# Widening the base product of a LoRA-MoE kernel from two groups of four batches to all eight batches at once

## The chip, the cores and the metric

The kernel runs on one core of one Trainium2 chip. The metric is the time of one execution on the device, in microseconds (us). Times of several runs are given as a median with the lowest and the highest.

In the profile PE is TensorE (matrix products), PEld its loads of the stationary operand, DVE is VectorE, ACT is ScalarE, POOL is GpSimd and SP is SyncE, which issues most DMAs (SPq is its queue). An instruction is named by its line of the kernel, its engine and operation, and the tile it writes and the tiles it reads.

## The reference, cut to what matters

Eight batches of 256 tokens with 1024 features go through a matrix that each batch chooses for itself, and then through a base layer with a mixture of low-rank adapters; the input is added at the end.

```python
def reference(x, ids, cond_weight, base_W, base_b, router_W, router_b, A, B, expert_map):
    y = einsum('bsi,boi->bso', x, cond_weight[ids])          # (8, 256, 1024), own 1024x1024 matrix per batch
    base_out = einsum('btd,od->bto', y, base_W) + base_b     # one 1024x1024 matrix for all
    probs = softmax(einsum('btd,nd->btn', y, router_W) + router_b)   # 15 choices
    topk_p, topk_i = top_k(probs, 8)
    w = einsum('btk,btke->bte', topk_p, onehot(expert_map[topk_i], 8))
    h = einsum('btd,erd->bter', y, A)                        # 8 experts of rank 16: 128 values
    lora = einsum('bter,eor->bto', h * w[..., None], B) * 2.0
    return x + base_out + lora
```

All data is fp32.

## The kernel before

Both large products are computed with Winograd's form of Strassen's scheme: a product of two 2x2 block matrices with seven block products in place of eight, at the price of sums and differences of blocks.

**Stage 1** (lines 265 to 540) makes y = x times the chosen matrix, one batch per round `b`. In a round one level of the scheme is used: seven calls of `block` (L287), each of four matmuls with 512 columns, into the PSUM tiles `pa`, `pb` and `pc`. `turns` (L388) makes the differences of x on VectorE, `first_sum` to `fourth_sum` those of the weights. Results are evicted into `m0` and `m1` (views of the buffer `late`), turned in 32x32 blocks by `flip` (L242, VectorE), and brought into their place in `y` by `moves` (L299): 16 copies on ScalarE for each of `m0` and `m1`. In a round the copies of `m0` run at once; those of `m1` are put in the deque `behind` and run in the next round. `project(b - 1)` (L129) computes the router's logits and h of the batch before: 16 matmuls with `y` as stationary operand, then a list of VectorE and ScalarE steps (`logits`, `softmax`, `top`, two `route_to`, `weigh`), whose result is `hw`; `turn` (L250) carries it into `hwT` with 16 ScalarE copies. `prepare` (L325) makes the block sums of the base matrix and stores them in DRAM as `left_raw` and `left_sum`; `load_left(n)` (L206) loads the n-th of seven sets back into two tiles of the pool `wpool`, which has eight.

**Stage 2** (lines 545 to 818) makes base_out + lora + x with two levels of the scheme. The outer level has seven products, each of which is an inner level of seven blocks. The batches are taken in two groups `g` of four; in each group the outer quarters of y are (half of the features) x (two batches), and an inner quarter has 256 tokens: one batch. So there are 14 products, each called through `product` (L597), and each of their matmuls has 256 columns.

A product issues seven blocks in a fixed order, `pa` (a11 b11), `pc` (s1 t1), `pa` (s2 t2), `pb` (a12 b21), `pa` (s3 t3), `pc` (s4 b22), `pa` (a22 t4), where blocks two, four, six and seven also take a matmul with the adapter term (`up`, `hwT`) in four of the seven products. After a block, `take` evicts the accumulator with its base added (on VectorE, or on ScalarE with the bias `bb` where there is no base) or `plus` adds it to an earlier result. The tiles `pa`, `pb` and `pc` have two buffers of one PSUM bank each. In the last product `pa` is split over two tiles, `pa` and `pe`, one for each half of the rows.

Ahead of each block stands a `gap(n)`: steps listed for it in `gaps`, and then `fill(2)`, which takes two steps from the deque `soon`, or from `later` if `soon` is empty. These deques carry VectorE's side work: the four `differences` (L218) of the next product, the outer sums (`first_terms`, `outer`), the joint sums, and the additions of the residual x with the stores of results. Within a stage PE, VectorE, ScalarE and SP issue in the order in which the program is written; a wait of one instruction holds all behind it on its engine. How the end of stage 1 and the start of stage 2 are interleaved on one engine is left to the scheduler.

The outer terms of a group are made out of place: `t2` is a tile of its own. `load_left` is called in gap 5, two products ahead. The projection of batch 7 stands between the second and the third product, in the tile `pe`.

Of the kernel before, what the change touches and what calls it, by code (L numbers as in the profile page):

```python
# [28 lines left out]
def kernel(  # L29
# [4 lines left out]
    xr: bass.AP,  # L34
    ids: bass.AP,
# [23 lines left out]
    assert ER == P and E == 8 and B % GB == 0  # L59
# [4 lines left out]

    tpool = ctx.enter_context(tc.tile_pool(name="t", bufs=6))
# [24 lines left out]
    yv = [y.rearrange("p i h j q k s -> p i h q j k s") for y in ys]  # L90
# [10 lines left out]
    v = late[:, lo : lo + 8 * S].rearrange("p (i j k t) -> p i j k t", i=2, j=2, k=2)  # L101
# [27 lines left out]
    def project(b, ph, order=(0, 1)):  # L129
# [4 lines left out]
        for j in order:  # L134
            for k in range(KC):
                nc.tensor.matmul(  # L136
                    ph[:, j, : ER + N],
                    lhsT=y[:, k // KH, th, k % KH // 2, bi, k % 2, ts(j, P)],
                    rhs=ar_sb[:, k, :],
                    start=(j == order[0] and k == 0),  # L140
                    stop=(k == KC - 1),
                    skip_group_check=True,
                )
# [73 lines left out]

    def differences(right):  # L218

        b11, b12, b21, b22 = right[:, 0, 0], right[:, 0, 1], right[:, 1, 0], right[:, 1, 1]  # L220
        t = {}

        def minus(n, of, less):
            def run():
                t[n] = tpool.tile([P, 2 * S], F32, name="tt").rearrange(
                    "p (k o) -> p k o", k=2
                )
                x, y = (t[v] if isinstance(v, int) else v for v in (of, less))
                nc.vector.tensor_sub(t[n], x, y)
                return t[n]  # L230

            return run

        return [minus(1, b12, b11), minus(2, b22, 1), minus(3, b22, b12), minus(4, b21, 2)]


    lefts = [0, 1, 3, 5, 4, 6, 2] * (B // GB)
# [27 lines left out]
    with ExitStack() as phase:  # L265
        xpool = phase.enter_context(tc.tile_pool(name="x", bufs=2))
        prep = phase.enter_context(tc.tile_pool(name="prep", bufs=1))
        ps = phase.enter_context(
# [30 lines left out]
        def moves(b, oh, m):  # L299


            y = ys[b // GB][:, oh, b % GB // 2, b % 2].rearrange(
# [132 lines left out]
        for b in range(B):  # L435
# [30 lines left out]
            def by_s4():  # L466
# [3 lines left out]
                run(moves(b, 0, m0))  # L470
# [47 lines left out]
            else:  # L518
                left[0] = load_left(lefts[0])
                terms = [step() for step in differences(yv[0][:, 0, 0])]  # L520
# [8 lines left out]
                left[1] = load_left(lefts[1])  # L529
# [3 lines left out]
            behind = moves(b, 1, m1)  # L533
# [11 lines left out]
    with ExitStack() as phase:  # L545

        mpool = phase.enter_context(tc.tile_pool(name="m2", bufs=1))
        qpool = phase.enter_context(tc.tile_pool(name="q2", bufs=6))
        xpool = phase.enter_context(tc.tile_pool(name="x2", bufs=1))
        places_x = [xpool.tile([P, 2, S], F32, name=f"xt{n}") for n in range(2)]  # L550
        places_x += [
            ms[:, o, h].rearrange("p (m t) -> p m t", m=2) for o in range(2) for h in range(2)
        ]
        loaded = 0
        ps = phase.enter_context(
            tc.tile_pool(name="ps", bufs=2, space=bass.MemoryType.PSUM)
        )
        ps_e = phase.enter_context(
            tc.tile_pool(name="ps_e", bufs=1, space=bass.MemoryType.PSUM)
# [4 lines left out]
        add, sub = nc.vector.tensor_add, nc.vector.tensor_sub  # L564


        soon, later = deque(), deque()
        steps_of = steps

        def fill(n):  # L570
            for _ in range(n):
                if soon or later:
                    soon.popleft()() if soon else later.popleft()[1]()

        def block(acc, left, right, first, up=None, hw=None):

            for mi in range(2):
                for k in range(2):
                    nc.tensor.matmul(  # L579
                        acc[mi][:, mi, :],  # L580
                        lhsT=left[:, 2 * k + mi, :],
                        rhs=right[:, k, :],
                        start=(first and k == 0 and (mi == 0 or acc[0] is not acc[1])),
                        stop=(up is None and k == 1),
                        skip_group_check=True,
                    )
                if up is not None:
                    nc.tensor.matmul(  # L588
                        acc[mi][:, mi, :],
                        lhsT=up[:, ts(mi, P)],  # L590
                        rhs=hw,
                        start=False,
                        stop=True,
                        skip_group_check=True,
                    )

        def product(left, terms, right, base, into, done, gaps, u=None, hw=None, split=False):  # L597
# [6 lines left out]
            b11, b12, b21, b22 = right[:, 0, 0], right[:, 0, 1], right[:, 1, 0], right[:, 1, 1]  # L604
            t1, t2, t3, t4 = terms

            def plus(dst, acc, other):
                if acc[0] is acc[1]:
                    add(dst, acc[0], other)  # L609
                else:  # L610
                    for mi in range(2):
                        add(dst[:, mi], acc[mi][:, mi], other[:, mi])

            def take(dst, acc, i, j):
                if isinstance(base, int):
                    for mi in range(2):
                        c = base + 2 * i + mi
                        nc.scalar.activation(  # L618
                            dst[:, mi], acc[mi][:, mi], AF.Identity, bias=bb[:, c : c + 1]
                        )  # L620
                else:
                    plus(dst, acc, base(i, j))

            def term(i, j):
                if u is None:
                    return ()
                if (i, j) == (0, 1):
                    return upd[:, u, :], hw[:, 1, :]
                return up[:, u, i, :], hw[:, j, :]

            def gap(n):
                for step in gaps.get(n, ()):
                    step()
                fill(2)

            pa = 2 * [ps.tile([P, 2, S], F32, name="pa")]
            pb = 2 * [ps.tile([P, 2, S], F32, name="pb")]
            pc = 2 * [ps.tile([P, 2, S], F32, name="pc")]
            if split:

                pa[1] = ps_e.tile([P, 2, S], F32, name="pe")
# [4 lines left out]
            gap(1)  # L646
# [5 lines left out]
            gap(3)  # L652
            block(pb, a12, b21, True, *term(0, 0))
            plus(c[0, 0], pb, c[0, 0])
# [3 lines left out]
            plus(c[1, 1], pa, c[1, 1])  # L658
            done(1, 1, c[1, 1])
            gap(5)  # L660
            block(pc, s4, b22, False, *term(0, 1))
            plus(c[0, 1], pc, c[0, 1])
            done(0, 1, c[0, 1])
            gap(6)
# [3 lines left out]
            fill(len(soon))  # L668
            while later and later[0][0] not in (c[0, 1], c[1, 0]):
                later.popleft()[1]()  # L670
            done(1, 0, c[1, 0])

        def fresh(i, j):
            return qpool.tile([P, 2, S], F32, name="q")
# [4 lines left out]
        for g in range(B // GB):  # L679
            y, hw = yv[g], hwTs[g]  # L680
            end = g == B // GB - 1
            b11, b12, b21, b22 = y[:, 0, 0], y[:, 0, 1], y[:, 1, 0], y[:, 1, 1]
            u = mpool.tile([P, 2, 2, 2, S], F32, name="u")
            t2 = mpool.tile([P, 2, 2, 2, S], F32, name="t2")
            xs = {}

            def number(oh, th, i, j):
                return ((g * 2 + oh) * 2 + th) * 4 + 2 * i + j

            def load_x(*r):  # L690
                nonlocal loaded
                xs[r] = places_x[loaded % len(places_x)]
                loaded += 1
                nc.sync.dma_start(xs[r].rearrange("p m t -> p (m t)"), xr[number(*r)])

            def finish(oh, th):


                def done(i, j, q):
                    x, n = xs[oh, th, i, j], number(oh, th, i, j)  # L700

                    def run():
                        add(q, q, x)
                        nc.sync.dma_start(outq[n], q.rearrange("p m t -> p (m t)"))

                    later.append((q, run))

                return done

            def joint(i, j, q):  # L710


                def run():
                    add(q, v[:, i, j], q)

                soon.append(lambda: add(u[:, i, j], u[:, i, j], q))
                later.append((q, run))
                finish(1, 1)(i, j, q)

            def last(i, j, q):  # L720
                if (i, j) == (1, 0):
                    for mi in range(2):
                        nc.sync.dma_start(outq[number(1, 0, 1, 0), :, ts(mi, S)], q[:, mi])
                else:
                    finish(1, 0)(i, j, q)

            def at(t):
                return lambda i, j: t[:, i, j]

            def update(dst, x, z, quarters=((0, 0), (0, 1), (1, 0), (1, 1))):  # L730
                return [
                    (lambda i=i, j=j: sub(dst[:, i, j], x[:, i, j], z[:, i, j]))
                    for i, j in quarters
                ]

            def first_terms(*quarters):

                for q in quarters:
                    soon.extend(update(b11, b12, b11, [q]))
                    soon.extend(update(t2, b22, b11, [q]))  # L740

            seven = [

                (b11, 0, at(u), nothing),
# [139 lines left out]
```

## Time and profile before

| | |
|---|---|
| median of 3 runs | 433.87 us (433.84 to 434.34) |
| the profiled execution | 434.09 us, of which the profile's span is 432.3 us |
| TensorE busy | 426.6 us, 99% of the span |
| VectorE busy | 328.6 us, 76% |
| ScalarE busy | 167.0 us, 39% |
| DMA | 106.05 MB, mean 245 GB/s |
| stage 2 on TensorE | from 228.23 us to the end |

The span is shorter than the execution's time, since something lies around it. A matmul record's duration holds its way through the array as well, so the spacing of records, and not their duration, tells what they cost. A row of the timeline or the chain has start, duration, engine, line, operation and count; in square brackets stands how long the engine was idle before and what ended it. In the groups by form the columns after the bar are busy us, mean ns of one, and idle time before.

### The profile page before, as it was taken

Reading aid. Unit: us, or ns where it says so; the run is one execution under the profiler, and the core shown is the slowest. Engines: PE = TensorE matmul, PEld = TensorE weight load, DVE = VectorE, ACT = ScalarE, POOL = GpSimd, SP = SyncE. Lnnn points to the kernel's source line nnn. Section 1 sums busy time; section 2 is a strip of 40 time slices with the busy share of each in tenths; the row PEclk is TensorE's granted clock in tenths of the full one; section 3 lists DMA queues with packets and bytes.
Section 4 is the critical chain, followed back from the end, with each engine's and each line's share of the span. In section 5 each row is a group of like instructions: output and inputs, shape, how many; then the busy total and the mean of one; then the engine's idle time right before and its main releaser. Section 6 shows DMA issues by size and latency. Waiting matters only on the chain.

```text
span 432.3 us, 4927 instructions
## 1 busy us (share of the span) xinstructions
PE 426.6 (99%) x1642; PEld 293.6 (68%) x1642; DVE 328.6 (76%) x556; ACT 167.0 (39%) x458; POOL 0.7 (0%) x6
## 2 busy tenths in 40 slices
PE   8999999999999999999999999999999999999997
PEld 5344464644646446455458898888888888888886
DVE  0699999986878898998885777946597858745595
ACT  1019377965758657776838231200201100000200
POOL 0000000000000000000000000000000000000000
DMA  7996997869687598792759942523967725912843
GB/s 265 416 351 264 345 331 294 303 223 324 217 299 281 208 338 312 257 316 86 242 231 371 370 143 104 201 91 110 378 211 273 284 73 202 392 48 69 296 159 133
DMA packets 32779, 106.05 MB, mean 245 GB/s; under 512 B 3058, under 2 KB 6898, under 8 KB 29554
## 3 DMA queue, kind: packets, MB, share of 16 engines
q1 hardware_dynamic: 32610, 105.21, 66.9%
q10 hardware_dynamic: 144, 0.52, 0.4%
q8 instruction: 13, 0.21, 0.2%
q14 instruction: 12, 0.10, 0.1%
HBM read 84.49 MB, written 21.23 MB: 245 GB/s over the span
## 4 chain that ended last, share of the span: by engine, by line
PE 96%; DMA 2%; SPq 1%; issue 0%; DVE 0%
PE pa L290 24%; PE pa L579 22%; PE pc L290 13%; PE pc L579 11%; PE pb L290 7%; PE ph L136 6%; PE pb L579 6%; PE pc L588 3%; DMA wt<-in_wq_dram 2%; PE pb L588 2%; PE pa L588 1%; PE pe L136 1%; PE pe L579 1%; SPq L359 0%; DMA ids_sb<-in_ids_dram 0%
## 5 line engine op out<-in xcount | busy, mean ns | idle before, releaser
L308 ACT COPY y<-late 32x256 f32<-32x256 f32 x256 | 103.0, 402 | 41.9 <-DVE late L244 38.9
L579 PE MATMUL pa<-tt,wt 128*128 128x256 f32 x324 | 78.1, 380 | 0.0
L579 PEld LDWEIGHTS pa<-tt,wt 128*128 128x128 f32 x324 | 61.3, 190 | 8.9 <-DVE u L609 0.3
L290 PE MATMUL pa<-wt,x 128*128 128x512 f32 x128 | 57.5, 593 | 0.4 <-DMA wt<-in_wq_dram 0.4
L290 PE MATMUL pa<-wt,tt 128*128 128x512 f32 x120 | 54.0, 593 | 0.0
L618 ACT ACTIVATE q<-pa,bb 128x256 f32<-128x256 f32 x12 | 5.0, 471 | 104.9 <-PE pa L579 104.0
L290 PEld LDWEIGHTS pa<-wt,x 128*128 128x128 f32 x128 | 24.2, 190 | 30.7 <-issue 30.4
L290 PEld LDWEIGHTS pa<-wt,tt 128*128 128x128 f32 x120 | 22.3, 190 | 26.1 <-issue 25.9
L255 ACT COPY hwT<-late 32x64 f32<-32x64 f32 x128 | 31.1, 243 | 18.7 <-DVE late L244 17.1
L136 PEld LDWEIGHTS ph<-late,y 128*128 128x128 f32 x224 | 28.4, 189 | 3.3 <-issue 3.3
L290 PE MATMUL pb<-wt,x 128*128 128x512 f32 x64 | 29.1, 595 | 1.0 <-DMA wt<-in_wq_dram 1.0
L290 PE MATMUL pc<-wt,x 128*128 128x512 f32 x64 | 28.9, 594 | 0.0
L290 PE MATMUL pc<-wt,tt 128*128 128x512 f32 x64 | 28.8, 592 | 0.0
L136 PE MATMUL ph<-late,y 128*128 128x143 f32 x224 | 28.6, 284 | 0.0
L579 PE MATMUL pc<-tt,wt 128*128 128x256 f32 x112 | 27.8, 379 | 0.0
L405 DVE TENSOR_TENSOR wt<-wt 128x2048 f32<-128x2048 f32 (+1 forms) x9 | 18.4, 2047 | 7.9 <-PE pa L290 5.5
L579 PE MATMUL pc<-y,wt 128*128 128x256 f32 x96 | 24.0, 379 | 0.0
L579 PE MATMUL pb<-y,wt 128*128 128x256 f32 x96 | 24.0, 379 | 0.0
L290 PEld LDWEIGHTS pb<-wt,x 128*128 128x128 f32 x64 | 12.0, 190 | 17.0 <-issue 14.4
L579 PEld LDWEIGHTS pc<-tt,wt 128*128 128x128 f32 x112 | 21.3, 190 | 2.9
L290 PEld LDWEIGHTS pc<-wt,x 128*128 128x128 f32 x64 | 12.1, 190 | 15.5 <-issue 14.8
L290 PEld LDWEIGHTS pc<-wt,tt 128*128 128x128 f32 x64 | 12.1, 190 | 15.3 <-issue 14.6
(118 smaller groups left out, 548.4 us busy)
## 6 DMA issues: line engine op xcount, KB each, us to landing
wt<-in_wq_dram SPq DMA_DIRECT2D x28, 1024.0 KB, 5.6
wt<-left_raw SPq DMA_DIRECT2D x14, 1024.0 KB, 6.2
wt<-left_sum SPq DMA_DIRECT2D x14, 768.0 KB, 7.9
out_dram<-q SPq DMA_DIRECT2D x31, 256.0 KB, 2.3
x<-in_xq_dram SPq DMA_DIRECT2D x7, 1024.0 KB, 6.9
late<-in_xr_dram SPq DMA_DIRECT2D x20, 256.0 KB, 6.7
wt<-in_wq_dram SPq DMA_DIRECT2D x8, 512.0 KB, 7.9
spare<-in_bq_dram SPq DMA_DIRECT2D x4, 1024.0 KB, 5.0
```

The source lines that it names most:

```text
L136: nc.tensor.matmul(ph[:, j, : ER + N], lhsT=y[:, k // KH, th, k % KH // 2, bi, k % 2, ts(j, P)], rhs=ar_sb[:, k, :], start=(j == order[0] ...
L255: lambda a=a, r=r: nc.scalar.copy(to[32 * r : 32 * r + 32, :, a, :], hw[32 * a : 32 * a + 32, :, ts(r, 32)],)
L290: nc.tensor.matmul(acc, lhsT=right[:, k, :], rhs=left[:, k, :], start=(first and k == 0), stop=(k == KH - 1), skip_group_check=True,)
L308: lambda a=a, r=r: nc.scalar.copy(y[32 * r : 32 * r + 32, :, :, a, :], m[32 * a : 32 * a + 32, :, :, r, :])
L405: nc.vector.tensor_add(q["s1"][:, h], q["a21"][:, h], q["a22"][:, h])
L579: nc.tensor.matmul(acc[mi][:, mi, :], lhsT=left[:, 2 * k + mi, :], rhs=right[:, k, :], start=(first and k == 0 and (mi == 0 or acc[0] is n ...
L588: nc.tensor.matmul(acc[mi][:, mi, :], lhsT=up[:, ts(mi, P)], rhs=hw, start=False, stop=True, skip_group_check=True,)
L618: nc.scalar.activation(dst[:, mi], acc[mi][:, mi], AF.Identity, bias=bb[:, c : c + 1])
```

## The change

Stage 2 takes all eight batches at once. The outer quarters are now (half of the features) x (four batches), an inner quarter has 512 tokens (two batches), and there are 7 products whose matmuls have 512 columns. The layout of y puts two batches of an inner quarter next to each other (256 elements each) so that a quarter is one run of 512 for each k. Five further things follow or go with it:

- The outer sums are made in place in y: T2 = b22 - b12 + b11 in b12, T3 = T2 - b11 in b11, T4 = b21 - T2 in b21, then b22 - T2 in b12. The order of the outer products changes accordingly, and so do where their results lie (`u`, `v`) and at which of them the bias enters: in the fifth product it is added with the base in one `scalar_tensor_tensor` for each half.
- PSUM: `pa` has two buffers of two banks, `pb` and `pc` have one of two banks each.
- The differences use tiles of `wpool` (two in one tile) in place of a pool of their own. The four of the first product, issued in stage 1's last round, have 1024 elements in place of 512.
- In the last round of stage 1 only ten of the sixteen copies of `m0` run at once. The other six and the sixteen of `m1` run in gaps 1, 2 and 3 of the first product (6, 5 and 11), and the projection of batch 7 stands in gap 5 of the first product, in the second `pa` buffer. The `turn` copies of batches 6 and 7 run in gap 0 of the third product.
- `load_left` is called in gap 0 of the product before. Residuals come in pieces of 512 KB into three tiles; each is asked for (`ask`) when an earlier one has been added. The last block is issued as 512 columns for the first half of the rows and twice 256 for the second, and evicted and stored in those three pieces.

The diff, cut to its core:

```diff
-    yv = [y.rearrange("p i h j q k s -> p i h q j k s") for y in ys]
+    yv = [y.rearrange("p h j i k b s -> p h j i k b s") for y in ys]
...
-                t[n] = tpool.tile([P, 2 * S], F32, name="tt").rearrange(
-                    "p (k o) -> p k o", k=2
-                )
+                if n % 2:
+                    t["two"] = wpool.tile([P, KH, OH], F32, name="wt")
+                t[n] = t["two"][:, ts((n - 1) % 2, 2)]
...
-    lefts = [0, 1, 3, 5, 4, 6, 2] * (B // GB)
+    lefts = [0, 1, 3, 4, 6, 5, 2]
...
-                run(moves(b, 0, m0))
+                behind.extend(moves(b, 0, m0))
+                run(behind, 10 if last else None)
...
-                terms = [step() for step in differences(yv[0][:, 0, 0])]
+                terms = [step() for step in differences(yv[0][:, 0])]
...
-                left[1] = load_left(lefts[1])
...
+        W = 2 * S
...
+        def block(acc, left, right, first, up=None, hw=None, pieces=(1, 1)):
             for mi in range(2):
+                for n in range(pieces[mi]):
+                    at = ts(n, W // pieces[mi])
+                    for k in range(2):
+                        nc.tensor.matmul(
+                            acc[:, mi, at],
+                            lhsT=left[:, 2 * k + mi, :],
+                            rhs=right[:, k, at],
...
+                    else:
+                        nc.vector.scalar_tensor_tensor(
+                            dst[:, mi], acc[:, mi], c, base(i, j)[:, mi], ALU.add, ALU.add
                         )
...
+        def gap(n, more=0):
             for step in gaps.get(n, ()):
                 step()
+            fill(3 if more and u is not None else 2)
...
+            pa = ps_a.tile([P, 2, W], F32, name="pa")
+            pb = ps_b.tile([P, 2, W], F32, name="pb")
+            pc = ps_b.tile([P, 2, W], F32, name="pc")
...
+            if end is not None:
+                fill(len(soon) + len(later))
+                block(pa, a22, t4, False, *term(1, 0), (1, 2))
+                end(pa)
+                return
...
+        def end(pa):
+            dst = u[:, 1, 0]
+            for mi, cut in ((0, ds(0, W)), (1, ds(0, S)), (1, ds(S, S))):
+                add(dst[:, mi, cut], pa[:, mi, cut], dst[:, mi, cut])
+                nc.sync.dma_start(
...
+        b11, b12, b21, b22 = (y[:, h] for h in range(2) for y in yv)
+        hw1, hw2 = hwTs
+        seven = [
+            (b11, None, 0, at(u), nothing),
+            (b21, at(u), None, fresh, finish(0, 0), 0, hw1),
+            (b12, at(u), None, at(u), nothing),
+            (b22, at(u), None, at(v), nothing, 2, hw2),
+            (b11, at(u), KH, at(u), nothing),
+            (b12, None, None, fresh, joint, 1, hw2),
+            (b21, at(u), None, at(u), finish(1, 0), 1, hw1),
+        ]
+        sums = {
+            0: update(b12, sub, b22, b12, [0]) + update(b12, add, b12, b11, [0]),
+            2: update(b11, sub, b12, b11),
+            3: update(b21, sub, b21, b12) + update(b12, sub, b22, b12),
+        }
+        def project_last():
+            ph = ps_a.tile([P, 2, W], F32, name="pa")[:, 0].rearrange("p (j o) -> p j o", j=2)
+            (logits, *rest), last_waiting = project(B - 1, ph)
+            soon.appendleft(logits)
+            soon.extend(update(b12, sub, b22, b12, [1]) + update(b12, add, b12, b11, [1]))
+            soon.extend(rest)
...
+            if not last:
+                gaps[0].append(lambda m=n + 1: left.update({m: load_left(lefts[m])}))
...
+            if n == 0:
+                for k, count in ((1, 6), (2, 5), (3, 11)):
+                    gaps[k].append(lambda count=count: run(behind, count))
+                gaps[5].append(project_last)
+            if n == 1:
+                gaps[0] += 3 * [ask]
+                ps_a.tile([P, 2, W], F32, name="pa")
+            if n == 2:
+                gaps[0].append(lambda: run(turn(*waiting)))
+                gaps[0].append(lambda: run(turn(*last_waiting)))
```

## The prediction, made before the changed kernel was run

> **What bounds the kernel now.** I read the page first (busy times and the chain that ended last), then the chain in order of time, the busy times by stage, the waits of the weight loads, the groups with shapes kept apart, and last the timelines of single engines round the edit.
>
> ```profile
> span 432.3 us, 4927 instructions
> ...
> PE 426.6 (99%) x1642; PEld 293.6 (68%) x1642; DVE 328.6 (76%) x556; ACT 167.0 (39%) x458; POOL 0.7 (0%) x6
> ...
> PE 96%; DMA 2%; SPq 1%; issue 0%; DVE 0%
> ```
>
> TensorE is busy 99% and carries 96% of the chain. Nothing else sets the end, so a gain must come out of PE's own instructions, its few stalls, or the tail.
>
> ```profile
> 220.88 3.43 PE pa L290 x8
> 224.31 3.92 PE ph L136 x32
> 228.23 1.73 PE pa L579 x8
> ```
>
> This is the chain in order of time (start, us, what) where stage 1 ends. Eight records of a matmul with 512 columns take 3.43 us, eight with 256 take 1.73. Stage 2, the part that is rewritten, begins at 228.23.
>
> ```profile
> core 0: us, PE busy (x) PEld busy (x) DVE busy (x) ACT busy (x) POOL busy (x), PEclk, DMA share, GB/s
> 228.23:429.30 201.07, 201.03 (x944) 176.58 (x943) 141.50 (x254) 29.88 (x88) 0.00 (x0) 1.00 0.56 206
> ```
>
> Busy times in stage 2: PE has no idle time, the clock is 1.00, VectorE is busy 141.5 of 201 us, the DMA engines 56%.
>
> ```profile
> PEld pa L579 <- DVE u L609: 0.3, 1, 0.3
> PEld pa L579 <- DVE late L609: 0.2, 1, 0.2
> ```
>
> These are all the waits of PE's loads in stage 2: 0.5 us, both behind VectorE evictions. In the PE timeline three blocks are late by 0.07, 0.10 and 0.08 us for them, 0.25 in all.
>
> **The change on PE.** Every matmul is two records. Before, stage 2 has 14 products of 28 matmuls (784 records) and eight products with 8 extra matmuls (128 records): 912 records of 256 columns. The second product runs from 240.15 to 255.69, 72 records, so 0.2158 us each: 196.8 us. After, there are 7 products on twice the columns: 456 records, of which the last half block is cut in two: 450 of 512 columns and 12 of 256. A stage-1 round has 56 records of 512 columns from 112.82 to 136.85 without its projection, 0.4291 each. Sum 193.1 + 2.6 = 195.7. The pairing saves 1.1 us and no more: the array's work is the same. The projection of batch 7 (3.93 us from 255.69) moves from between two products into the first product and costs the same. Before, 201.04 us of chain minus 3.93 and 196.8 leaves 0.31 of stalls and seams; after, if nothing stalls, PE ends at 228.23 + 3.93 + 195.7 = 427.9 instead of 429.27: 1.4 less.
>
> **What the other engines must deliver.** A block is 3.43 us, or 5.15 with the outer-term matmuls; call the products P0 to P6. P0 with the projection runs 228.2 to 256.2, P1 to 287.1, P2 to 311.1, P3 to 342.0, P4 to 366.0, P5 to 396.9, P6 to 427.9.
>
> ```profile
> L579 PEld LDWEIGHTS pa<-tt,wt 128*128 128x128 f32 x324 | 61.3, 190 | 8.9 <-DVE u L609 0.3 <-DVE late L609 0.2
> L405 DVE TENSOR_TENSOR wt<-wt 128x1024 f32<-128x1024 f32 x2 | 2.5, 1225 | 2.4 <-DMA wt<-in_wq_dram 2.3
> ```
> ```profile
> 230.72 0.69 DVE L732 TENSOR_TENSOR t<-y 128x512 f32<-128x512 f32 x1
> 231.33 0.68 DVE L732 TENSOR_TENSOR y<-y 128x512 f32<-128x512 f32 x1
> ```
>
> Weight loads (190 ns in the groups by form) already hide in a 216 ns record, so halving them gains nothing. VectorE starts independent 512-wide operations 0.61 us apart; with 512 elements more at the slope between 685 ns (512) and 1225 ns (1024), a 1024-wide one occupies 1.14, or 1.25 when it needs the one before. Stage 2 after has 41 evictions (four takes and three additions in each of seven products, less the eight takes of P0 and P5 that ScalarE does), 24 differences, 20 in-place outer sums (16 such units before), 8 joint sums, 16 residuals: 109 units, 124 us against 129 for some 214 half-size ones now. All of it lies beside PE if the order fits: three units per 3.43 us block are 3.42, four per 5.15 us block are 4.6. I replayed the queue. P2 is tightest: last take of P1 to 288.4, two differences 290.8, take 291.9 (wanted at 293.9), two more, a take, two sums, take 298.9 (wanted at 300.8), addition 305.5 (wanted at 307.7). So 1.9 us of cover; without it each late microsecond is a microsecond of PE. In P4 the take becomes two scalar_tensor_tensor of 512, an operation without a row: I take 0.65 each from the 512-wide row, with 1.4 us of cover; at twice that it costs 0.8 us. Below nothing is excluded: no PE instruction waits for a take that comes earlier.
>
> Moved steps. The four first differences, in stage 1's last round, grow from 0.61 to 1.14 each: VectorE is then 2.2 us later from 213, and its 2.00 us idle before 217.55 (PE's third-sum block) takes that up. Their two wpool tiles come free at 207 to 211 by PE's blocks; if one comes from the a21 tile (read until 217.4), the last block of stage 1 waits 1.3 us.
>
> ```profile
> 223.12 6.61 ACT L308 COPY y<-late 32x256 f32<-32x256 f32 x16 [7.83 <-DVE late L244]
> ...
> 231.72 0.84 ACT L618 ACTIVATE u<-pc,bb 128x256 f32<-128x256 f32 x2 [0.46 <-PE pc L579]
> ...
> 234.31 5.78 ACT L308 COPY y<-late 32x256 f32<-32x256 f32 x14
> ```
>
> Batch 7's projection now needs all its copies on ScalarE (0.413 us apart). Ten of the first sixteen stay before 228; takes with bias grow to 0.55 per half. Take to 232.5, 6 copies 235.0, take 236.1, 5 copies 238.1, take 239.3, 11 copies 243.9. PE asks at 245.4: 1.5 us of cover. The projection's tile is the second pa buffer; its logits (249.5) and copy are read long before P1 writes there (256.2). The 32 turn copies (7.8 us) in P2 are wanted only in P3. On SP, each load_left moves from gap 5, two products ahead, to gap 0 of the product before its own, and waits there until PE ends the product that held its tiles. Behind the one in P1 three residual loads are queued, first wanted 23 us later. Its pair lands in 6.2 and 7.9 us by the page and has a product, 24 us, to do so; I cost it at nothing, and without that cover PE would wait those 8 us. Stores leave SP behind their additions as before. In P6 one residual load is asked for 3 us before its addition and may hold VectorE about 1 us; the next eviction wanted has 3 us.
>
> **The tail.**
>
> ```profile
> 428.04 0.41 DVE L612 TENSOR_TENSOR q<-pa,u 128x256 f32<-128x256 f32 x1
> 428.57 1.51 SPq L723 DMA_DIRECT2D out_dram<-q  x2
> 428.66 0.59 PE L588 MATMUL pe<-hwT,up 128*128 128x256 f32 x2
> 429.29 0.42 DVE L612 TENSOR_TENSOR q<-pe,u 128x256 f32<-128x256 f32 x1 [0.84 <-PE pe L588]
> ```
>
> Now the two last evictions come from two tiles, pa and pe, and only the second follows PE's end; from its end (429.71) to the end of the span are 2.6 us. After, the last two pieces lie in one PSUM bank. In the row at 231.72 ScalarE waits 0.46 us for the whole block though its half was written 0.9 us before. The Trainium skill (PSUM — Partial Sum Buffer, Terms, "PSUM bank") has it that no engine may read a bank while TensorE writes it. By the rule both pieces are evicted after PE's end, 0.39 us more (spacing of two such evictions at 423.72 and 424.11) and 0.05 on SP; without it the tail stays. I take 0.44, as the row waits so; from below 0, from above 1.3, if even the other bank's 512 columns wait.
>
> **Sum.** Minus 1.4 on PE plus 0.44 is minus 0.95: a span of 431.35. The profiled execution took 434.09, of which 432.3 is span; it would be 433.15. The median of the runs, 433.87, lies 0.2 below it, so I forecast 432.95.
>
> A rule against it: the skill's Perfetto Trace Analysis, Optimizing Scalar/DVE Operations, says that where these engines are not saturated but cause bubbles, breaking instructions up lets work finish sooner. This change does the opposite, with single pb and pc buffers in place of two. By the rule each hand-over is 0.5 us later (1.14 against 0.61), four in each of seven products, 15 us at most, a time of 448; by the replay every one lies in 1.4 us or more of cover, and costs nothing. I take the replay.
>
> **The rivals.** (a) VectorE becomes the pace. For it: three units fill a block without rest. Against: the queue is empty in most late gaps, and 1.35 us per unit would be needed to eat P2's cover. At 1.5 us P2, P3 and P4 stall 2.0, 1.4 and 1.6 us: about 438. With small losses, or the 1.3 us of the a21 tile, it is 433.5 to 434.5.
>
> (b) Slower outright, in stage 1. The new layout puts batches b and b + 1 in turns of 256 elements in one range of y.
>
> ```profile
> 107.21 6.61 ACT L308 COPY y<-late 32x256 f32<-32x256 f32 x16 [0.30 <-DVE late L244]
> ```
> ```profile
> 108.90 4.08 PE L136 MATMUL ph<-late,y 128*128 128x143 f32 x32
> ```
>
> In odd rounds the projection of b - 1 starts at 108.9 while the copies of b run until 113.8. Before, they touch separate ranges. If waits are kept by range and not by run, it waits 4.9 us in rounds 1, 3 and 5 and 3 us in round 7: 17.7 us, some 450. It decides if any such wait is drawn at all; against it, the two sets of runs have one step and never meet.
>
> (c) The saving is not had, because 512-column records take longer beside these operands: then only the tail is left, 434.3 at most. Stage 1 has the same shape under a VectorE as busy, so this is small.
>
> **How the numbers follow.** What a measurement of this kernel can tell from no change is about 0.2%, 0.87 us. Forecast case 0.64, own range 432.4 (tail free) to 433.4: it straddles that bound, 0.51 faster and 0.13 within. Rival (a) 0.24: 0.08 within, 0.16 slower. Rival (b) 0.08, slower. Rival (c) 0.04: 0.02 within, 0.01 slower, 0.01 faster. That is 0.52, 0.23, 0.25. The range runs from 432.3 to 437.0 and leaves out (b), the worst of (a) and a little below.
>
> **What would show it.** Right: matmul records in stage 2 halved, 8 of them in 3.43 us; PE ending near 427.9; no weight-load wait over 0.3 us; two 256-wide evictions after PE's end. Wrong: PE gaps behind VectorE in P2 or P4 (a), projections of even batches starting 3 to 5 us late behind ScalarE (b), or the one in P0 waiting for copies.

## The result: slower, for a wait that the sum did not have and a tail that it took too short

The changed kernel takes 435.87 us (median of 6 runs, 435.63 to 437.16) against 434.01 for the kernel before (6 runs): a ratio of 1.0046, interval 1.0033 to 1.0059. It is slower by 1.9 us where a gain of 0.9 was forecast. The profiled execution took 436.10 us, with a span of 434.3.

The page of the changed kernel (span, busy times, chain by engine):

```profile
span 434.3 us, 3771 instructions
...
PE 425.8 (98%) x1192; PEld 208.8 (48%) x1192; DVE 323.5 (74%) x453; ACT 162.6 (37%) x438; POOL 0.7 (0%) x6
...
PE 93%; DMA 3%; DVE 2%; SPq 1%; issue 1%; DVEq 0%; ACT 0%
```

TensorE does 450 records fewer and its weight loads fell from 68% to 48% of the span, but it now holds 93% of the chain where it held 96%. The chain now passes through other engines at two places. Their shares are no measure of the cost: behind the first place the chain runs back over a DMA (4.07 us in the first row below) beside a TensorE that was busy until 228.43. The cost is read from TensorE's own waits. The first place is where stage 2 starts, in the chain in order of time (start, us, what):

```profile
225.21 4.07 DMA left_raw<-spare
229.28 0.35 ACT late L155
229.63 0.04 issue
229.68 3.70 PE pa L581 x8
233.38 3.43 PE pc L581 x8
```

and in the waits of TensorE (waiting instruction, what it waited for, total us, times, longest):

```profile
PE pa L581 <- ACT late L155: 1.2, 1, 1.2
```

The first block of the first product stands behind ScalarE's copy of h (L155) out of `ph`, the projection of batch 6, although it neither reads h nor writes where `ph` lies. Before, it followed the projection at once. The block itself then takes 3.70 us where the next takes 3.43, so the stop costs another 0.27 us (called the restart below).

The second is the tail. In the chain TensorE ends the first half of the rows at 426.99 and the whole at 429.59:

```profile
426.13 0.86 PE pa L590 x2
429.14 0.45 PE pa L590 x2
```

The timeline shows what follows (the number in brackets is idle time before, and what ended it):

```profile
428.98 0.59 PE L590 MATMUL pa<-hwT,up 128*128 128x256 f32 x2
429.61 1.35 DVE L736 TENSOR_TENSOR u<-pa,u 128x512 f32<-128x512 f32 x3 [2.68 <-PE pa L590]
430.33 1.31 SPq L737 DMA_DIRECT2D out_dram<-u  x3
```

All three last evictions start after TensorE's end, though the first of them reads a half that was finished 2.6 us earlier. VectorE stood idle for 2.68 us before. From TensorE's end (429.59 by the chain) to the end of the span are 4.7 us, against 3.0 in the kernel before (429.27 to 432.3).

The two spans compare as follows; each row is a difference of after and before, in us.

| Piece | forecast | measured |
|---|---|---|
| stage 1, until the projection of batch 6 ends (228.23 before, 228.43 after) | 0 | +0.20 |
| wait and restart at the first block (1.25 and 0.27) | 0 | +1.52 |
| stage 2 on TensorE without them (201.04 before, 199.64 after) | -1.40 | -1.40 |
| from TensorE's end to the end of the span | +0.44 | +1.68 |
| sum | -0.95 | +2.00 |

The 0.20 is there at 13.04 before and 13.23 after, where matmuls still wait for their first weights, far from any edit. It wanders from profile to profile: in one of the kernels below stage 2 starts 0.36 us earlier than in the kernel before.

### The profile page after: what moved, and what is told of

Same layout as the page of the kernel before. It is cut to its first block, busy times and chain, and to the rows that moved or that the text cites. A ratio compares the mean times of both kernels' runs of the same rounds, so it can differ in the third digit from the quotient of the medians.

```text
span 434.3 us, 3771 instructions
## 1 busy us (share of the span) xinstructions
PE 425.8 (98%) x1192; PEld 208.8 (48%) x1192; DVE 323.5 (74%) x453; ACT 162.6 (37%) x438; POOL 0.7 (0%) x6
## 4 chain that ended last, share of the span: by engine, by line
PE 93%; DMA 3%; DVE 2%; SPq 1%; issue 1%; DVEq 0%; ACT 0%
PE pa L294 23%; PE pa L581 22%; PE pc L294 12%; PE pc L581 11%; PE pb L294 7%; PE pb L581 6%; PE ph L135 5%; PE pc L590 3%; DMA wt<-in_wq_dram 2%; PE pa L590 2%; PE pb L590 2%; DMA left_raw<-spare 1%; PE pa L135 1%; SPq L363 0%; DMA ids_sb<-in_ids_dram 0%
## 5 line engine op out<-in xcount | busy, mean ns | idle before, releaser
L581 PE MATMUL pa<-wt 128*128 128x512 f32 (+1 forms) x172 | 76.3, 582 | 0.0
L581 PEld LDWEIGHTS pa<-wt 128*128 128x128 f32 x172 | 32.7, 190 | 39.9 <-issue 39.5
L614 ACT COPY q<-pa 128x1024 f32<-128x1024 f32 x3 | 3.0, 1012 | 114.7 <-PE pa L581 96.9
L581 PE MATMUL pa<-y,wt 128*128 128x512 f32 x56 | 25.3, 594 | 1.2 <-ACT late L155 1.2
L581 PE MATMUL pc<-wt 128*128 128x512 f32 x56 | 25.8, 592 | 0.0
L581 PE MATMUL pb<-y,wt 128*128 128x512 f32 x56 | 25.8, 592 | 0.0
L581 PE MATMUL pc<-y,wt 128*128 128x512 f32 x56 | 25.8, 592 | 0.0
L247 DVE STREAM_TRANSPOSE late<-late 128x512 f32<-128x512 f32 (+1 forms) x33 | 21.3, 647 | 1.1
```

The costliest lines, as they stand in the source:

```text
L247: nc.vector.transpose(half, of)
L581: nc.tensor.matmul(acc[:, mi, at], lhsT=left[:, 2 * k + mi, :], rhs=right[:, k, at], start=(first and k == 0), stop=(up is None and k == 1 ...
L614: nc.scalar.copy(dst, acc)
```

## The experiments

Two theories. **Theory 1**: the wait at the start belongs to the PSUM pool, not to data. `pa` is one pool of two buffers in banks 4 to 7; the first product's `pa` lies in banks 4 and 5, where stage 1's `pc` was, and `ph` lies in bank 6. The first tile of the pool waits for the last reader of every old tile in the pool's whole range. (The banks follow from the order in which pools and tiles are opened; the profile does not print them.) **Theory 2**: waits between matmuls and evictions are kept for a whole tile. Rivals stand with the runs.

### Two pools of one buffer

```diff
-        ps_a = phase.enter_context(
-            tc.tile_pool(name="ps_a", bufs=2, space=bass.MemoryType.PSUM))
+        ps_a = [phase.enter_context(
+            tc.tile_pool(name=f"ps_a{n}", bufs=1, space=bass.MemoryType.PSUM)) for n in range(2)]
+        turns_a = deque([0, 1, 1, 0, 1, 0, 1, 0, 1])     # which pool each pa tile comes from
...
```

> The two buffers of pa come from two PSUM pools of one buffer each (banks 4-5 and 6-7), nothing else is changed; P0 still uses banks 4-5, which the last pc tiles of stage 1 held, and not bank 6, where the projection ph lies. Theory 1 (the first tile of a pool waits until every old tile within the pool's whole range is read, so P0's first block waits for ScalarE's copy of h out of ph): the wait of PE on ScalarE at the start of stage 2 (1.2 us in the changed kernel's profile) is gone, PE ends 1.2 us earlier, time 434.6. Rival (the wait belongs to something that the first product really needs from ScalarE, such as its copies into y): the wait stays, time 435.9.

Measured: 434.38 us (13 runs), 1.0009 of the kernel before (1.0001 to 1.0017). The timeline of TensorE at the start of stage 2:

```profile
225.78 2.49 PE L135 MATMUL ph<-late,y 128*128 128x143 f32 x19
228.11 3.59 PE L589 MATMUL pa<-y,wt 128*128 128x512 f32 x8
231.54 3.60 PE L589 MATMUL pc<-wt 128*128 128x512 f32 x8
```

No idle time stands in brackets: the block follows the projection, and its eight records take no longer than the next. From the projection's end (228.27 in the chain) to TensorE's end (427.92) are 199.65 us. The tiles lie in the banks they had before; only the pools' ranges differ. Theory 1 stands, and the wait was worth 1.5 us of the median.

### Two tiles in the last product

```diff
+            if end is not None:
+                pa, cut = (pa, ps_a.tile([P, 2, W], F32, name="pa")), (1, 2)
...
-            block(pa, a11, b11, True)
+            block(pa, a11, b11, True, pieces=cut)     # each pa block: pieces 1 and 2 into pa[0], 3 into pa[1]
...
-                add(dst[:, mi, cut], pa[:, mi, cut], dst[:, mi, cut])
+                t = pa[n // 2]
+                add(dst[:, mi, cut], t[:, mi, cut], dst[:, mi, cut])
```

> In the last product the accumulator pa is spread over two tiles: columns up to three quarters in one, the last quarter (half of the rows' second half, 256 columns) in the other. Each pa block is issued in the three pieces of the last one. Theory 2 (an eviction waits for all matmuls of its tile, so that all three last evictions and 512 KB of stores start only after PE's end): the first two evictions now start 1.3 us before PE's end, one of 256 columns is left behind it, and from PE's end to the end of the span are 3.0 to 3.3 us in place of 4.7; time 434.2 to 434.5. Rival (the tail is long because half a megabyte is stored at the end, whoever waits): from PE's end still 4.3 us or more, time 435.5 or more. The wait at the start of stage 2 stays at 1.2 us by both.

Measured: 434.65 us (10 runs), 1.0018 (1.0009 to 1.0027). The tail in its timeline:

```profile
427.90 1.02 DVE L749 TENSOR_TENSOR u<-pa,u 128x512 f32<-128x512 f32 x2 [1.39 <-PE pa L591]
428.57 0.59 PE L591 MATMUL pa<-hwT,up 128*128 128x256 f32 x2
428.62 1.36 SPq L750 DMA_DIRECT2D out_dram<-u  x3
429.20 0.42 DVE L749 TENSOR_TENSOR u<-pa,u 128x256 f32<-128x256 f32 x1 [0.27 <-PE pa L591]
```

Two evictions now run before TensorE's end, and one of 0.42 us is left behind it. The first of the two reads a half that TensorE ended at 426.57, but starts only at 427.90, just behind the second piece of its tile (427.87). From TensorE's end (429.18) the span lasts 3.4 us in place of 4.7; 3.0 to 3.3 were expected, and the time is 0.15 us above its expected range. The same half megabyte is stored, so the rival, which asked for 4.3 or more, falls. The wait of 1.2 us at the start is still there, as it should be.

### Both

> Two pools for pa and two tiles for pa in the last product. If the two causes are separate and are all there is: minus 1.2 and minus 1.4 to 1.7, time 433.0 to 433.3, faster than the kernel before by 0.7 to 1.0 us, which is what pairing the matmuls saves (1.1). Rival (the pairing has a third cost, hidden behind these two): 433.8 or more.

Measured: 433.04 us (18 runs), 0.9981 (0.9974 to 0.9988). The two waits are separate: singly they gave 1.5 and 1.2 us, together 2.8. In the profile stage 2 starts at 227.87 and TensorE ends at 427.55: 199.7 us against 201.0.

```profile
227.87 3.43 PE pa L590 x8
427.10 0.45 PE pa L599 x2
```

What is left against the kernel before is a gain of 0.9 us: the 1.4 on TensorE that the pairing was to bring, less 0.4 in a tail that is still longer (3.4 us against 3.0), and what stage 1 wanders by. That this is the 0.9 of the forecast is in part luck, since the forecast's 0.44 in the tail stood for another wait.

### One tile, written in turn

```diff
-                block(pa, a22, t4, False, *term(1, 0), (1, 2))
-                end(pa)                                  # three evictions after all matmuls
+                block(pa, a22, t4, False, *term(1, 0), (1, 2), end)   # eviction after each piece
```

> One tile as in the changed kernel, but the last block is written in turn: the matmuls of a piece, then its eviction and its store, then the next piece. If waits are kept by bank or by range, the first eviction (its own bank) starts 2.5 us before PE's end and the tail is some 3.2 us: time 434.4. If they are kept by tile (theory 2), the second piece's matmuls also wait for the first eviction, and the third's for the second: PE stands still for 0.9 and 0.6 us, and the time is 435.6 to 436.6.

Measured: 436.33 us (5 runs), 1.0060 (1.0047 to 1.0073). Its timeline:

```profile
426.73 0.69 DVE L736 TENSOR_TENSOR u<-pa,u 128x512 f32<-128x512 f32 x1
...
427.47 1.13 PE L581 MATMUL pa<-wt 128*128 128x256 f32 x4 [0.78 <-DVE u L736]
...
429.07 0.42 DVE L736 TENSOR_TENSOR u<-pa,u 128x256 f32<-128x256 f32 x1 [1.65 <-PE pa L590]
429.55 1.13 PE L581 MATMUL pa<-wt 128*128 128x256 f32 x4 [0.52 <-DVE u L736]
```

The second piece goes into another bank than the one that the first eviction reads, and still TensorE waits 0.78 us for it. So what is kept apart is the tile, not the bank. Writing the pieces in turn only moves the wait onto TensorE.

### h copied first

```diff
+            nc.scalar.copy(t["h"], ph[:, :, :ER])
             nc.vector.tensor_add(lg, ph[:, :, ER : ER + N], ...)
 ...
             nc.scalar.activation(t["ex"], lg, AF.Exp)
-            nc.scalar.copy(t["h"], ph[:, :, :ER])
```

> The changed kernel with one line moved: in logits ScalarE copies h out of ph before the exponential, and not after it, so that the last read of ph ends at about 228.8 instead of 229.6 (the copy needs nothing from VectorE). Theory 1: PE's wait at the start of stage 2 shrinks with it from 1.2 to some 0.4 us, time 435.0. Rival (PE waits for ScalarE's place in its row for another reason): the same shrinking is possible here, but not a wait that follows the end of the h copy by the same 0.1 us as in the changed kernel.

Measured: 435.30 us (7 runs), 1.0030 (1.0019 to 1.0041). The wait changed its owner:

```profile
228.54 0.38 ACT late L148
228.94 0.20 DVE late L149
```
```profile
PE pa L581 <- DVE late L149: 0.7, 1, 0.7
```

Now VectorE's addition of the logits reads `ph` last: it ends at 229.15; TensorE starts at 229.19. The size was missed (0.4 expected, 0.69 measured), because VectorE's addition is itself made to wait for ScalarE's copy (L148) and begins only at 228.94. Why one reader of `ph` waits for the other is not shown. But that the wait goes over to another engine speaks for theory 1: what counts is the last read of `ph`, whoever does it. In the changed kernel, too, TensorE started 0.05 us after that read.

### The kernel before, with its two pools in the other order

```diff
-        ps = ...   # banks 0 to 5
-        ps_e = ... # bank 6, where ph was
+        ps_e = ... # bank 0
+        ps = ...   # banks 1 to 6
```

> The kernel before with the two PSUM pools of stage 2 opened in the other order and nothing else: ps_e takes bank 0, and ps the banks 1 to 6, so that its range covers bank 6 with the projection ph; the first product's pa lies in bank 1, which is free long before. Theory 1 (range of the pool): the kernel before now shows the same wait of PE on ScalarE, 1.2 us, time 435.2. Rival (the wait comes from wider tiles, from the deferred copies or from another part of the change): no wait, 434.0.

Measured: 437.04 us (6 runs), 1.0070 (1.0051 to 1.0089). Nothing of the change is in this kernel, and the wait is there, at a `pa` in bank 1:

```profile
PE pa L579 <- ACT late L156: 2.1, 1, 2.1
```

It is 2.1 us and not 1.2, since here ScalarE does all sixteen copies ahead of the h copy, which ends at 230.16 and not at 229.62; that step was left out of the expectation. Whether the old tile's own place counts or that of the whole pool it came from, the runs do not separate. In the profiled run (436.29 us) it explains the loss. The six runs lie in two groups, 435.8 to 436.3 and 437.8 to 438.0; the upper three show a granted clock of 0.995 to 0.996 and the lower three 0.999 to 1.000, but whether that is the cause is not shown.

### Three tiles in the last product

Each piece of the last product's `pa` gets a tile and a pool of its own, on top of the kernel with both mends.

> As the kernel with two pools and two tiles, but pa of the last product lies in three tiles of three pools (512, 256 and 256 columns), so that the first eviction and its 256 KB store leave 2.6 us before PE's end, the second 1.3 us before. Theory 2 with stores: the last 0.4 us of the tail (3.4 against 3.0 us in the kernel before) come from 512 KB issued within 2 us; now the tail is 3.0 us and the time 432.6. Rival (the 0.4 us are not the stores): no change, 433.0.

Measured: 432.89 us (8 runs), 0.9975 (0.9965 to 0.9985). The 256 KB store leaves earlier:

```profile
425.16 0.69 DVE L772 TENSOR_TENSOR u<-z,u 128x512 f32<-128x512 f32 x1
425.82 0.59 PE L614 MATMUL z<-hwT,up 128*128 128x256 f32 x2
425.88 2.66 SPq L773 DMA_DIRECT2D out_dram<-u  x3
```

and its eviction starts 2.6 us before TensorE's end, as soon as its own tile is written. But from TensorE's end (427.73) to the end of the span (431.1) it is 3.4 us, as with two tiles. So the stores ahead were not what made the last 0.3 to 0.4 us. By the DMA rows of the two profiles the last byte moves about 1.4 us after the last eviction's end in the kernel before and here alike (429.71 to 431.1, and 428.17 to 429.5). The difference lies behind that byte, where the span goes on for 1.2 us before and 1.6 here; what fills it is open. This kernel and the one with two tiles can't be told apart (their intervals overlap); both beat the kernel before, by 0.8 and 1.1 us by their ratios, and so the changed one.

## Why the prediction was wrong, point by point

**The step that failed first: stage 2 starts at 228.23 as before.** The time lies inside the range that was stated, 432.3 to 437.0, but by luck: the upper part of that range stood for VectorE as the pace, and that did not happen. The sum ran "if nothing stalls", and the moved projection was looked at only where P1 writes onto its tile. What P0's own first tile has to wait for was not asked. The tile's banks would have given no wait; the pool's range did, 1.25 us and 0.27 for the restart. The two-pool kernel and the kernel before with swapped pools show it from both sides.

**The step that failed second: the tail.** "I take 0.44, as the row waits so" was the wrong reading of a right row. At 231.72 ScalarE waits for the whole block though its half is written; that was put down to the bank, as the Trainium skill has it (PSUM — Partial Sum Buffer, Terms, "PSUM bank"). In that row bank and tile are the same, so it could not tell them apart. In the changed kernel a tile has two banks, and the tile decides: matmuls waited 0.78 us for an eviction from another bank of their tile. Whether the page's rule holds within one bank no run here can tell, since the tile would give the same waits. The case that happened, the other bank's 512 columns waiting too, was the prediction's bound of 1.3, and the measured 1.68 lies even above it: VectorE's end came 0.93 us later relative to TensorE's (three evictions), and the rest is the last stores, whose last byte moves some 0.4 us later behind VectorE's end, and the 0.3 to 0.4 us that stay open.

**Right: the pairing's saving.** -1.40 on TensorE as forecast, and -1.36 to -1.39 in the kernels that do not wait (199.68 and 199.65): 1.1 from 2.5 ns per pair of records, the rest from stalls that are gone. TensorE's weight loads waited twice for new differences (L232), 0.2 us each, and the matmuls themselves show no idle time there. Rival (c) falls.

**Right: VectorE does not become the pace.** 1024-wide operations follow each other 1.14 us apart as worked out, P2 to P6 show no wait of a matmul on them, so neither rival (a) nor the rule on larger instructions weighed in the prediction took effect inside stage 2. The scalar_tensor_tensor takes 0.74 us and two of them 1.32, where 1.30 was taken:

```profile
347.30 1.40 DVE L623 SCALAR_TENSOR_TENSOR u<-pa,bb,u 128x512 f32<-128x512 f32 x2
348.62 1.21 DVE L232 TENSOR_TENSOR wt<-y 128x1024 f32<-128x1024 f32 x1
```

**Right: the moved projection fits.** ScalarE's last copies end at 246.27, and TensorE asks at 247.1 (a row of the timeline and one of the chain):

```profile
241.73 4.54 ACT L312 COPY y<-late 32x256 f32<-32x256 f32 x11
247.11 3.92 PE pa L135 x32
```

The cover is 0.8 us and not 1.5. The plan had the first take end 0.8 us after its block (at 232.5), although its own pair of 0.55 makes 1.1. In the run ScalarE was free again 1.4 us after the block (233.38 to 234.75), and the two later pairs kept it 1.15 and 1.29 us.

**Right: no waits in stage 1 (rival b).** The projection follows its block in all odd rounds, in the chain at 109.26 for instance (109.06 before), though batches now lie in turns.

So the term on TensorE was right within 0.1 us, and both misses lie at a seam (the start and the end of the new stage), where the plan's waits are set by how memory is handed out.

## What to carry to other kernels

When a stage gets new accumulators, ask for each pool which old tiles lie in its whole range and when the last of them is read; a pool that covers one late tile makes its first user wait, wherever that user's own buffer lies, and splitting the pool in two cost nothing here. An eviction that is meant to overlap the rest of its accumulation needs a tile of its own, not just a bank of its own. The saving of 1.4 us is smaller than the one seam of 1.5, so the start and the end of a rewritten stage deserve the same replay as its inside.

## What was not expected of the hardware

A stop of TensorE costs more than the wait itself. After the wait at the first block eight records took 3.70 us where the next eight took 3.43, so 0.27 us on top. It does not grow with the wait: the 3.70 is the same after 0.69 us (h copied first) and after 1.25, and in the kernel before with swapped pools it is 1.99 against 1.73 us after 2.06. What makes it up was not taken apart; the first weights, too, are loaded only when the wait ends (229.68 in the changed kernel).
